# Layer 0's experts: slots of 256 rows at fixed places, then each expert's rest

## The chip, the cores and the metric

The kernel runs on one core of a Trainium2 chip. The metric is the device time of one execution in microseconds; 1060.14 us is the median of three runs before the change (1055.96 to 1061.04). TensorE is called PE, VectorE DVE, ScalarE ACT, GpSimd POOL and SyncE SP. Loads from device memory are issued mostly by SP, small stores by ACT, and transfers whose addresses come from a list of row numbers (indirect ones) by POOL.

## The reference

There are 3327 rows of 256 numbers, a symmetric 0/1 adjacency matrix, and two layers. Each layer is a graph step followed by a mixture of experts, and both are added to the rows. What is computed, cut to what matters here (`ln` is a layer normalisation):

```python
# layer 0
h = ln(x); a = (adj == 1)
x = x + (a @ h / a.sum(1)) @ W.T + b
h = ln(x)
probs = softmax(h @ gate_w + gate_b)                 # 16 experts
top_p, top_i = top_k(probs, 2); top_p /= top_p.sum(-1)
for each row and each of its two experts e:
    x += top_p * ((silu(h @ w1[e]) * (h @ w2[e])) @ w3[e])   # 256 -> 512 -> 256
# layer 1: a graph attention step, then 6 experts with a router of two layers, again 2 a row
```

Every row thus goes through two of the 16 experts: 6654 pairs of a row and an expert.

## The kernel before

The 3327 rows are 26 row tiles of 128 (the last one has 127). Seven chunks of four row tiles (the last has two) are the unit of all that follows the graph product.

**Graph step.** `graph` goes through blocks of chunks: 12, 8, 4 and 2 row tiles in each of the two layers (`GRAPH`). For each block it loads the adjacency matrix in groups (`load_adj`, L647 and L650: one row tile by the block's columns for wide blocks, three or six row tiles for narrow ones), makes a 0/1 mask of it on DVE (`mask_of`, L658), and multiplies (L772) into PSUM banks, two for each chunk. Three loads and three masks can be ahead (`AHEAD`). When a block is done its chunks are finished in steps (`finish`): multiplication with W (L715), layer normalisation, storing the rows (`store`) and the normalised rows, transposes (L732), the router (`choose`, L798) and `dispatch`. These steps are handed out over the groups of the next block, `steps` (7) for each chunk, two chunks at a time (`in_turn`). The last block's steps come after all matmuls.

**Lists.** `dispatch` picks two experts a row and writes the row's number and weight into that expert's list in device memory with indirect scatters (L361, two for each row tile). Its place is the number of earlier rows with that expert, kept in `seen`. Unused places of a list point to a spare row with weight zero. On one chunk of each layer a scatter waits until the one before the last has landed.

**Slots of layer 0.** A slot is 128 places of one expert's list. `slot_table` works out on DVE which expert and which place each slot has. Nine early slots need only the first block's rows; their table is made when the third block begins (`routed0`). The other 52 have a table made after the last chunk's `dispatch`. So 61 slots (`USUAL0`) are run in any case, and a branch (`asked`, `more`) leads to more of them when these don't suffice. For each slot SP reads a place from the table and loads 128 list entries (`places`, L543: `who`), POOL gathers the rows (`rows_in`, L551: `xg`), PE transposes them (`turned`, L568), then computes the hidden layer in 16 matmuls (`hidden0`, L938, two records each in the profile), ACT and DVE form silu times product (L942, L946), PE computes the output in four matmuls (`out0`, L954, eight records), DVE applies the row's weight (L957: `y`), and POOL adds the rows to the array in device memory (`rows_added`, L575: `xd`). Adds wait for each other. Weights are in two sets of buffers, one for even and one for odd slots; a slot loads its expert's weights (L536) only if its expert differs from that of the slot before last. `slots0` issues all this, gathers four slots ahead.

**The switch to layer 1.** Over the last eight slots `head1` reads back the first six row tiles and normalises them; `graph1_ahead` loads six groups of adjacency early. The remaining rows are read back (L1011) after the last add.

**Order.** The order of each engine's instructions is made by the framework from the program's order, the dependencies and its own estimate of durations. Explicit constraints are set by `issue_after` and by added dependencies; `in_order` keeps SP's loads for the slots in program order. In the profile the early slots run interleaved with the last block of layer 0's graph.

## Time and profile before

| | us |
|---|---|
| median of three runs | 1060.14 |
| the profiled execution | 1051.82 |
| its span, first to last instruction | 1049.9 |
| PE busy | 955.7 (91%) |
| PE's weight loads busy | 832.9 (79%) |
| DVE busy | 502.1 (48%) |
| POOL busy | 423.0 (40%) |
| ACT busy | 264.4 (25%) |
| hidden matmuls of layer 0's slots (L938), 1952 records | 351.5 busy, 283 ns each |
| output matmuls of layer 0's slots (L954), 488 records | 115.5 busy, 380 ns each |
| graph matmuls (L772), 1456 records | 351.5 busy, 395 ns each |
| mean granted clock of TensorE | 0.956 |

A line of the page's groups gives a source line, engine, operation and tile, the count, the busy time and the mean duration of one, and then how long the engine stood idle before such instructions and what ended the wait. Matmuls are pipelined: one starts while the one before still drains, so durations overlap, and the distance between starts tells what a matmul costs in a stream. In a timeline, neighbouring instructions of one kind are merged into a line: start, time from the first start to the last end, line, shape, count, and in brackets an idle time before it with the instruction or transfer that ended it.

### The profile page before, as it was taken

How to read it: one execution, taken by the hardware profiler on the slowest of the kernel's cores; microseconds unless marked ns; L12 is line 12 of the kernel's file. 1: busy time of each engine (PE TensorE's matmuls, PEld its weight loads, DVE VectorE, ACT ScalarE, POOL GpSimd, SP SyncE). 2: the span in 40 equal slices, each digit the busy share in tenths (PEclk: the TensorE clock that was granted, in tenths of full speed). 3: DMA queues.
4: the chain of work that ended last, by engine and by line, in shares of the span. 5: the costliest groups of instructions: out<-in, count | busy, mean ns of one | idle time of the engine just before them, and what ended most of it. 6: DMA issues, size and time to landing. Idle time of an engine off the chain costs nothing. (4 is left out here: it accounts for less than half of the span.)

```text
span 1049.9 us, 17490 instructions
## 1 busy us (share of the span) xinstructions
PE 955.7 (91%) x5404; PEld 832.9 (79%) x5404; DVE 502.1 (48%) x1839; ACT 264.4 (25%) x556; POOL 423.0 (40%) x400
## 2 busy tenths in 40 slices
PE   7899999799799999999999889999898688999980
PEld 5678877599699999999999878877677467888870
DVE  6667569166311222221212658676585641444653
ACT  3310211123111111111111524231222233444430
POOL 2040064055434445444443211002450476777742
PEclk9999899899989999999999989999999879999996
DMA  9987685969775766668767469857946666332365
GB/s 339 313 305 235 241 233 155 290 196 246 188 211 115 184 155 176 195 154 204 183 152 193 110 216 316 271 182 221 236 108 203 223 185 189 92 97 91 96 231 204
DMA packets 114716, 208.23 MB, mean 198 GB/s; under 512 B 32018, under 2 KB 68370, under 8 KB 114620
## 3 DMA queue, kind: packets, MB, share of 16 engines
q1 hardware_dynamic: 74590, 157.33, 47.2%
q0 software_dynamic: 21040, 31.61, 13.7%
q10 hardware_dynamic: 18990, 18.14, 5.6%
q8 instruction: 44, 0.72, 0.3%
q14 instruction: 52, 0.43, 0.1%
HBM read 232.46 MB, written 35.92 MB: 256 GB/s over the span
## 5 line engine op out<-in xcount | busy, mean ns | idle before, releaser
L772 PE MATMUL acc<-big,y 128*128 128x512 f32 (+2 forms) x1456 | 351.5, 395 | 28.4 <-DVE big L658 18.8
L772 PEld LDWEIGHTS acc<-big,y 128*128 128x128 f32 (+1 forms) x1456 | 267.9, 196 | 84.4 <-DVE big L658 7.8
L938 PE MATMUL acc<-xT,w 128*128 128x128 f32 x1952 | 245.0, 283 | 1.7 <-DMA w<-in_ffn_w 1.6
L938 PEld LDWEIGHTS acc<-xT,w 128*128 128x128 f32 x1952 | 238.7, 198 | 2.6 <-PE acc L938 1.3
L361 POOL DMA_INDIRECT list<-where,t_idx x104 | 110.1, 1059 | 187.0 <-DVE t_idx L357 74.8
L575 POOL DMA_INDIRECT xd<-y,who x61 | 95.9, 1572 | 178.8 <-DMA xd<-y,who 69.7
L658 DVE TENSOR_SCALAR big<-adj 128x1536 fp32r<-128x1536 int32 (+8 forms) x136 | 111.4, 824 | 97.4 <-DMA adj<-in_adj_t 67.9
L551 POOL DMA_INDIRECT xg<-hd,who x119 | 119.0, 1000 | 81.8 <-issue 30.8
L946 DVE TENSOR_TENSOR hid<-hid,acc 128x512 f32<-128x512 f32 x61 | 41.9, 688 | 204.8 <-PE acc L938 200.3
L954 PE MATMUL acc<-w,hid 128*128 128x256 f32 x488 | 115.5, 380 | 1.4 <-DVE hid L946 1.4
L954 PEld LDWEIGHTS acc<-w,hid 128*128 128x128 f32 x488 | 88.0, 190 | 11.3 <-DVE hid L946 1.8
L1119 ACT ACTIVATE h<-acc,v 128x256 f32<-128x256 f32 x116 | 54.9, 474 | 98.8 <-PE acc L1116 97.7
L583 POOL DMA_INDIRECT zd<-y,who x58 | 69.8, 1204 | 24.7 <-DVE y L1133 12.7
L570 ACT COPY xT<-mm 128x256 f32<-128x256 f32 (+1 forms) x74 | 32.2, 435 | 186.4 <-PE mm L568 155.8
L1116 PE MATMUL acc<-xT,v 128*128 128x256 f32 x232 | 62.8, 394 | 2.6 <-DMA v<-w1d 2.0
L1116 PE MATMUL acc<-h,v 128*128 128x256 f32 x232 | 60.5, 383 | 0.6 <-ACT h L1119 0.6
L1131 DVE TENSOR_TENSOR y<-acc,v 128x512 f32<-128x512 f32 x29 | 20.1, 691 | 83.1 <-PE acc L1128 83.1
L1128 PE MATMUL acc<-v,h 128*128 128x256 f32 x232 | 58.1, 394 | 0.1
L942 ACT ACTIVATE hid<-acc 128x512 f32<-128x512 f32 x61 | 36.4, 597 | 84.5 <-PE acc L938 83.0
L268 POOL TENSOR_TENSOR ln_var<-ln_var,half 128x2 f32<-128x2 f32 (+2 forms) x19 | 15.2, 803 | 102.7 <-DVE ln_var L266 91.8
L957 DVE TENSOR_SCALAR y<-acc,who 128x256 f32<-128x256 f32 x61 | 29.5, 484 | 52.1 <-PE acc L954 51.0
L1116 PEld LDWEIGHTS acc<-xT,v 128*128 128x128 f32 x232 | 43.8, 200 | 11.8 <-ACT h L1119 4.0
(264 smaller groups left out, 914.4 us busy)
## 6 DMA issues: line engine op xcount, KB each, us to landing
w<-in_ffn_w SPq DMA_DIRECT2D x183, 512.0 KB
adj<-in_adj_t SPq DMA_DIRECT2D x66, 768.0 KB
adj<-in_adj_t SPq DMA_DIRECT2D x50, 512.0 KB
v<-w1d SPq DMA_DIRECT2D x7, 898.0 KB
hd<-ln_h ACTq DMA_DIRECT2D x12, 512.0 KB
z<-zd SPq DMA_DIRECT2D x6, 1024.0 KB
adj<-in_adj_t SPq DMA_DIRECT2D x8, 765.0 KB
w_all<-w1d SPq DMA_DIRECT2D x6, 898.0 KB
```

The lines of the kernel that those rows point to most:

```text
L361: ins = nc.gpsimd.indirect_dma_start(out=rows_of[2 * (t0 + j) + i], out_offset=bass.IndirectOffsetOnAxis(ap=idx[:, i, j : j + 1], axis=0), ...
L551: last["pool"] = nc.gpsimd.indirect_dma_start(out=xg[:, h, :], out_offset=None, in_=of, in_offset=bass.IndirectOffsetOnAxis(ap=who[:, h, 1 ...
L575: nc.gpsimd.indirect_dma_start(out=to, out_offset=bass.IndirectOffsetOnAxis(ap=who[:, 0, 0:1], axis=0), in_=y, in_offset=None, compute_op= ...
L583: last["z"] = nc.gpsimd.indirect_dma_start(out=zviews[n * s + h], out_offset=bass.IndirectOffsetOnAxis(ap=who[:, h, 0:1], axis=0), in_=y[: ...
L658: last["mask"] = nc.vector.tensor_scalar(mask[:kr, :, :cols], a[:kr, :, :cols], value, None, op0=op)
L772: last["graph"] = nc.tensor.matmul(acc[c][k][:, :w], y[:kr, j, part, k * P : (k + 1) * P], mask[:kr, jj, i0 : i0 + w], start=(j == 0 and p ...
L938: nc.tensor.matmul(q[:, c, :], w[:, k, h0 : h0 + 2 * P - 1 : 2], xT[:, k, :], start=(k == 0), stop=(k == KD - 1))
L946: last["silu"], last["hid"] = silu, nc.vector.tensor_mul(hid, hid, ps[1])
L954: last["slot"] = nc.tensor.matmul(ps[:, :D], hid[:, c, :], w3[:, c // 2, c % 2, :], start=(c == 0), stop=(c == NC0 - 1))
L1116: ins = nc.tensor.matmul(ps[:, c, :], w[:, k, c : H1 : NC1], src[:, k, :], start=(k == 0), stop=(k == 1))
L1119: last["act"] = nc.scalar.activation(dst[:, c, :], ps[:, c, :], AF.Relu, bias=w1s[s % 3][:, BB + 2 * i + c : BB + 2 * i + c + 1])
L1128: nc.tensor.matmul(ps[:, h, :], h2[:, c, h * P : (h + 1) * P], w[:, c, :], start=(c == 0), stop=(c == NC1 - 1))
```

## The change

The graph blocks of layer 0 become 12, 4 and 10 row tiles (`GRAPH0`); layer 1 keeps its blocks. The first block's finishing steps may run on into the third block (`over`), and the third block's finishing steps are handed out beside the first slots (`beside`) instead of after the matmuls.

Slots of layer 0 get 256 places. After the 16 row tiles of the first two blocks, `filled` raises every expert's count to at least 256, so that its first 256 places are closed; places without a row keep pointing to spare rows. The first eight slots are the first 256 places of experts 0 to 7, at addresses known when the program is built; their lists are asked for at the 22nd group of the third block. After the last `dispatch`, `rank_table` ranks experts 8 to 15 by count, and then 0 to 7. Each of the former gets a slot for its first 256 places and one for its rest, each of the latter one for its rest. The rest's slot has a width by the rank: 256, 224, 224, 192, 192, 192, 160 or 160 rows (`WIDTHS`). That makes 32 slots. `spill_table` works out whether any rest is larger than its width; then the branch is taken, to two more slots and, inside it, to the others.

Weights are loaded once for a run of slots of one expert, 24 runs in all, unconditionally; hidden weights of the next run when a run starts, output weights when their own run starts. Hidden layers are computed in two halves of 256 hidden units, with the previous slot's output between them. Each slot's two adds go out without waiting for each other; both wait for both adds of the slot before. Buffers: three for `xg`, three half-size ones for `hid`, two for `y` (each now 256 rows), where there were five, two and four. The wait of a list scatter for the one before the last is now set on all chunks of the last block. `head1` and the ahead-of-time loads of layer 1 move with the slots' new numbers.

```diff
+    GRAPH0 = [CHUNKS[:3], CHUNKS[3:4], CHUNKS[4:]]
+    NE0 = sum(map(len, CHUNKS[:4]))
+    assert NE0 <= NF and len(GRAPH0[2]) <= 3
+    SA = 2 * P
+    HALF = E0 // 2
+    WIDTHS = [SA, SA - 32, SA - 32, SA - 64, SA - 64, SA - 64, SA - 96, SA - 96]
+    assert len(WIDTHS) == HALF and NP % SA == 0
+    USUAL0 = 4 * HALF
+    LATE0 = USUAL0 - 5
+    FEW0 = USUAL0 + 2
+    SLOTS0 = USUAL0 + (2 * N + E0 * (SA - 1 - WIDTHS[-1])) // SA
...
+        if not second_softmax and blk is GRAPH0[1][-1]:
+            filled(seen)
...
-                if blk is GRAPH[1][-1] and len(issued) > 1:
+                if len(issued) > 1 and (blk is GRAPH[1][-1] if second_softmax else blk in GRAPH0[2]):
...
+    def filled(seen):
+
+        ps = ps_mm.tile([P, 512], F32, name="mm")
+        nc.tensor.matmul(ps[:, :E0], ones_h, seen, start=True, stop=True)
+        short = work.tile([P, 2, E0], F32, name="f_short", bufs=1)
+        for h in range(SA // P):
+            nc.vector.tensor_scalar(short[:, h, :], ps[:, :E0], -1.0, float(SA - h * P), op0=OP.mult, op1=OP.add)
+        for h in range(SA // P):
+            nc.vector.scalar_tensor_tensor(seen, short[:, h, :], slot_p[:, 0:1], seen, op0=OP.is_gt, op1=OP.add)
...
+    def rank_table(seen):
+
+        ps = ps_mm.tile([P, 512], F32, name="mm")
+        nc.tensor.matmul(ps[:, :E0], ones_h, seen, start=True, stop=True)
...
+        return out, rank, rest
+
+    def spill_table(rank, rest, head):
...
     def in_turn(those):
 
-        now, those = those[:2], those[2:]
-        while now:
-            for i, one in enumerate(list(now)):
+        now = []
+        while those or now:
+            while those and len(now) < 2:
+                now.append(those.pop(0))
+            for one in list(now):
                 try:
                     next(one)
                     yield
                 except StopIteration:
                     now.remove(one)
-                    now += those[:1]
-                    those = those[1:]
 
...
+    def graph(name, blocks, prepare, value, op, wx, update, after, steps, routed, between=None, pools=None, ahead=(), ready=None, over={}, finish_with=None):
...
+            for b, block in enumerate(blocks):
...
+                    if (b, gi) in routed:
+                        routed[b, gi]()
...
-                    for _ in range(-(-left // (len(groups) - gi))):
+                    for _ in range(-(-left // max(1, over.get(b, len(groups)) - gi))):
...
-                post, left = in_turn([finish(*p) for p in parts]), steps * len(parts)
-            for _ in post:
-                pass
+                if not left:
+                    assert next(post, None) is None and not those
+                    post = in_turn(those)
+                those += [finish(*p) for p in parts]
+                left += steps * len(parts)
+            (finish_with or list)(post)
...
+    plan = [(e, None, 0, 0, SA) for e in range(HALF)]
+    for r in range(HALF):
+        plan += [(HALF + r, "rank", r, 1, SA), (HALF + r, "rank", r, 2, WIDTHS[r])]
+    plan += [(2 * HALF + r, "rank", HALF + r, 2, WIDTHS[r]) for r in range(HALF)]
+    assert len(plan) == USUAL0
+    plan += [(3 * HALF + i, "spill", i, 1, SA) for i in range(SLOTS0 - USUAL0)]
+
+    def places0(s):
+
+        run, table, row, col, _ = plan[s]
+        who = io.tile([P, 2, 3], I32, name="who", bufs=16)
+        if table is None:
+            src = lists[0][run * NP : run * NP + SA, :]
+        else:
+            with in_order():
+                at = nc.sync.value_load(early[table][row : row + 1, col : col + 1], min_val=0, max_val=E0 * NP)
+            src = lists[0][bass.ds(at, SA), :]
+        with in_order():
+            last["who"] = nc.sync.dma_start(who, src.rearrange("(h p) w -> p h w", p=P))
+        return who
...
-        early["table"], early["had"] = slot_table(E0, seen0, P, slot_p, first=EARLY0)
-        for s in range(EARLY0):
-            who[s] = places(early["table"], s, E0, lists[0], P)
+        for s in range(HALF):
+            who[s] = places0(s)
...
+    def load0_hidden(s):
+        run, table, row, _, _ = plan[s]
+        if table is None:
+            which[run] = slice(run, run + 1)
+        else:
+            with in_order():
+                which[run] = bass.ds(nc.sync.value_load(early[table][row : row + 1, 0:1], min_val=0, max_val=E0 - 1), 1)
+        with in_order():
+            for i, w in enumerate((ffn0_w1, ffn0_w2)):
+                load0(s, i, w[which[run]].rearrange("o (p k) h -> p (o k) h", k=KD))
+
+    def load0_out(s):
+        with in_order():
+            load0(s, 2, ffn0_w3[which.pop(plan[s][0])].rearrange("o (a p b) d -> p (o a) b d", p=P, b=2))
...
+    def hidden0(s, xT, half):
+        n, ps = plan[s][-1], []
+        for w in w0[plan[s][0] % 2][:2]:
+            q = bank(half, [P, 2, SA])
+            for c in range(2):
+                for k in range(KD):
+                    h0 = half * 2 * P + c
+                    last["slot"] = nc.tensor.matmul(q[:, c, :n], w[:, k, h0 : h0 + 2 * P - 1 : 2], xT[:, k, :n],
+                                                    start=(k == 0), stop=(k == KD - 1))
             ps.append(q)
-        hid = io.tile([P, NC0, P], F32, name="hid", bufs=2)
-        silu = nc.scalar.activation(hid, ps[0], AF.Silu)
-        if s >= EARLY0 + 4 and packs:
+        hid = io.tile([P, 2, SA], F32, name="hid", bufs=3)
...
+    def out0(s, hid):
+        w3 = w0[plan[s][0] % 2][2]
+        ps = bank(2, [P, 2, D])
+        for h, m in parts0(s):
+            for c in range(NC0):
+                nc.tensor.matmul(ps[:m, h, :], hid[c // 2][:, c % 2, h * P : h * P + m], w3[:, c // 2, c % 2, :],
+                                 start=(c == 0), stop=(c == NC0 - 1))
+        y = io.tile([P, 2, D], F32, name="y", bufs=2)
+        names = []
+        for h, m in parts0(s):
+            nc.vector.tensor_scalar(y[:m, h, :], ps[:m, h, :], weight(who[s], h)[:m, :], None, op0=OP.mult)
+            ins = nc.gpsimd.indirect_dma_start(
+                out=xd_of[2 + h] if s < USUAL0 else xd,
+                out_offset=bass.IndirectOffsetOnAxis(ap=who[s][:m, h, 0:1], axis=0),
+                in_=y[:m, h, :], in_offset=None, compute_op=OP.add,
+            )
+            if s < USUAL0:
+                waits(ins, [v for g, v in enumerate(x_added.get(s - 1, ())) if g != h])
+                if s == 0:
+                    waits(ins, x_stored[: len(GRAPH0[0]) + len(GRAPH0[1])])
+                if s == HALF:
+                    waits(ins, x_stored[len(GRAPH0[0]) + len(GRAPH0[1]) :])
+                names.append(ins.ins.name)
+        x_added[s] = names
...
-    graph("0", prepare0, 1.0, OP.is_equal, Later(0), update0, after0, 7, routed0, (operands_early, derived, derived_late))
-
-    table0 = slot_table(E0, seen0, P, slot_p, taken=early["had"], two=True, low=seen_head, late=LATE0 - EARLY0)
...
     def slots0(first, end):
+        usual = not first
+        for s in range(first - 3, end + 1):
+            if usual and s in AHEAD_AT:
+                graph1_ahead(AHEAD_AT.index(s))
+            if usual and s == HALF - 3:
+                early["rank"], *early["ranks"] = rank_table(seen0)
+            if usual and s == HALF + 4:
+                early["spill"] = spill_table(*early["ranks"], seen_head)
+            if usual and s == end - 2:
+                early["more"] = asked(early["spill"], 0)
+            if s == first - 1:
+                load0_hidden(first)
+            if first <= s < end and starts(s):
+                if next_run(s) < end:
+                    load0_hidden(next_run(s))
+                load0_out(s)
+            known = HALF if s < HALF - 3 else end
+            for i in range(max(who, default=-1) + 1, min(s + 4, known)):
+                who[i] = places0(i)
+            for i in range(max(xg, default=-1) + 1, min(s + 3, known)):
+                xg[i] = rows_in0(i)
             if first <= s + 1 < end:
+                xT[s + 1] = turned0(s + 1, xg[s + 1])
             if first <= s < end:
+                hid[s] = [hidden0(s, xT[s], 0)]
+                if usual:
+                    head1(2 * (s - LATE0))
+                yield
+            if first <= s - 1:
+                out0(s - 1, hid.pop(s - 1))
             if first <= s < end:
+                hid[s].append(hidden0(s, xT.pop(s), 1))
+                if usual and s == end - 1:
+                    spare = const.tile([P, 1], F32, name="spare")
+                    nc.scalar.activation(spare, half[:, 0:1], AF.Exp, bias=hid[s][1][:, 0, 0:1], scale=0.0)
+                if usual:
+                    head1(2 * (s - LATE0) + 1)
+                yield
+            elif s == first - 1:
+                yield
...
+    slots = slots0(0, USUAL0)
+
+    def beside(post):
+
+        for i, _ in enumerate(slots):
+            for _ in range(3 if i == 0 else 2):
+                if next(post, slots) is slots:
+                    return
+
+    graph("0", GRAPH0, prepare0, 1.0, OP.is_equal, Later(0), update0, after0, 7, {(2, 21): routed0, (2, 25): lambda: next(slots)},
+          (operands_early, derived, derived_late), over={1: 19, 2: 20}, finish_with=beside)
...
     with more(*early["more"]):
-        slots0(USUAL0, SLOTS0)
+        list(slots0(USUAL0, FEW0))
+        with more(*asked(early["spill"], 0, 5, "many")):
+            list(slots0(FEW0, SLOTS0))
```

## The prediction

> **What bounds the kernel now.** I read the page's busy shares first (PE 955.7 us, 91%; no other engine above 48%), then the busy time by stage, then PE's timeline where a stage shows idle time, then the queue that PE waited for there. By stage (the first column after the stretch is its length, then each engine's busy time with its instructions, the granted clock, the DMA share and GB/s):
>
> ```profile
> core 0: us, PE busy (x) PEld busy (x) DVE busy (x) ACT busy (x) POOL busy (x), PEclk, DMA share, GB/s
> 90.00:212.00 122.00, 111.32 (x526) 90.64 (x525) 73.45 (x340) 18.99 (x40) 32.59 (x30) 0.92 0.71 223
> 212.00:281.00 69.00, 68.46 (x513) 65.17 (x513) 42.13 (x227) 20.77 (x36) 38.41 (x36) 0.99 0.78 221
> 281.00:292.00 11.00, 2.42 (x12) 2.00 (x11) 0.66 (x2) 0.37 (x1) 6.11 (x5) 0.68 0.74 195
> 292.00:602.00 310.00, 306.86 (x2227) 294.62 (x2226) 75.71 (x169) 59.82 (x121) 133.36 (x103) 0.99 0.66 169
> ```
>
> Up to 90 us layer 0's first graph block runs, which the change leaves alone; 90 to 212 is its second and third, 212 to 281 the fourth with the nine early slots mixed in, 292 to 602 the late slots. PE is full in the slots and has two holes. PE's timeline at the first, at the second, and over one late slot:
>
> ```profile
> 183.60 4.60 PE L772 MATMUL acc<-big,y 128*128 128x512 f32 x19
> 195.58 6.50 PE L772 MATMUL acc<-big,y 128*128 128x512 f32 x19 [7.39 <-DVE big L658]
> ...
> 279.85 1.89 PE L954 MATMUL acc<-w,hid 128*128 128x256 f32 x8
> 290.32 0.70 PE L568 MATMUL mm<-ident,xg 128*128 128x128 f32 x2 [8.57 <-DMA xg<-hd,who]
> ...
> 298.26 0.39 PE L568 MATMUL mm<-ident,xg 128*128 128x128 f32 x2
> ...
> 585.45 1.89 PE L954 MATMUL acc<-w,hid 128*128 128x256 f32 x8
> 587.17 0.39 PE L568 MATMUL mm<-ident,xg 128*128 128x128 f32 x2
> 587.40 3.93 PE L938 MATMUL acc<-xT,w 128*128 128x128 f32 x32
> 591.17 1.89 PE L954 MATMUL acc<-w,hid 128*128 128x256 f32 x8
> ```
>
> Starts matter here, since a busy matmul overlaps the next: a late slot is 5.72 us (585.45 to 591.17), 3.77 for 32 hidden records, 1.73 for 8 output records, 0.23 for the transposes. So a pass costs 0.118 us at 128 columns and 0.216 at 256. The first hole waits for a mask, thus for an adjacency load on SP, the second for a gather. SP's queue at the first (start, time over all, issues):
>
> ```profile
> 150.88 15.34 SPq L647 DMA_DIRECT2D adj<-in_adj_t  x6
> 176.45 11.35 SPq L543 DMA_DIRECT2D who<-list  x9
> 187.90 1.80 SPq L647 DMA_DIRECT2D adj<-in_adj_t  x3
> ```
>
> Nine row-list loads stand between two adjacency loads: they wait for the list scatters to land, and then take some 1.2 us each, because each reads its address from a table. For 22 us no adjacency load goes out.
>
> **The change part by part.** All against the profiled execution, 1051.82 us (span 1049.9 and 1.9 around it); the median of the three timed runs, 1060.14, is 0.8% above it.
>
> *Slots of 256 rows.* Before, 61 x 128 = 7808 rows. After, 16 x 256 + 2 x 1600 (the widths' sum) = 7296 rows in 32 slots. The reference's router on its own inputs gives 324 to 511 rows an expert; with the first 256 places filled up, the rests are 132 to 255 and 140 to 200 in the two halves, and each fits its rank's width (the tightest: 255 in 256). So the usual 32 slots suffice. Hidden: 61 x 3.77 = 230.0 us becomes 7296/256 x 32 x 0.216 = 197.0. Output: every slot has two halves and a half moves 256 columns whatever its rows, so 61 x 1.73 = 105.5 becomes 64 x 1.73 = 110.7. Transposes: 61 x 0.23 = 14.0 becomes 14.7. Sum -27.1 us, on PE's path. That hidden passes run at 0.216 with 256 moving columns is seen in layer 1, which has this shape already:
>
> ```profile
> 930.46 1.89 PE L1128 MATMUL acc<-v,h 128*128 128x256 f32 x8
> 932.19 1.03 PE L1116 MATMUL acc<-h,v 128*128 128x256 f32 x4
> 933.05 1.03 PE L1116 MATMUL acc<-xT,v 128*128 128x256 f32 x4
> ```
>
> Four in 0.86 us. [...]
>
> *The second hole goes.* Late slots' tables need the last row tiles' routing, and early slots are too few to cover it. The chain ran from the last index (261.67, DVE) to the transpose at 290.32: 28.6 us. The hole cost 8.57 idle, and the first slot after it took 7.94 instead of 5.72 at a low clock: 10.8 us. After, eight early slots of 10.83 us (32 x 0.216 + 2 x 1.73 + 0.46) stand there, and the last block's finishing runs beside them: 87 us of cover instead of 51.
>
> *The first hole goes.* Row lists for the early slots are asked for at group 21 of the last block, behind most adjacency loads, and from fixed addresses: 8 x 0.35 us instead of 9 x 1.2 and a table. It cost 7.39 idle and 19 matmuls at 6.50 instead of 4.60: 9.3 us.
>
> The three together: -47.2 us. Against that:
>
> *The early slots' lists.* They now need chunks 2 and 3, whose steps end together at group 15: 16 scatters of 1.28 us on POOL (0.97 and 0.3 before each), 20.5, then 2.9 to the list load, 4.1 to the gather, 6.4 to the transpose (the distances at 276.96, 279.87, 283.95, 290.32): 33.9 us. Cover: ten groups of 2.16 us, and 6.2 us of finishing matmuls (32 L715 records at 1.55 for 8). Between 0 and 12 us; I take 4, somewhat under the difference of 6.1, since the first of the scatters can go while the step's other chunk still computes. Adjacency loads behind the list loads on SP: 0 to 7.4 (the old hole), I take 1, since nine table reads are gone.
>
> *The rank table's chain.* 28.6 us before, against two early slots (21.7) by the order of issue, three (32.5) if PE's order is drawn out: 0 to 9 us with the low clock; I take 2.
>
> *POOL.* The wait of each list scatter for the one before the last, on 8 scatters before, is now on 20, in the queue that also gathers and adds. Eight such scatters took 17.1 us (229.87 to 246.97) instead of 10.2. The queue stood for DMA there:
>
> ```profile
> 234.42 0.97 POOL L361 DMA_INDIRECT list<-where,t_idx  x1 [2.21 <-DMA list<-where,t_idx]
> ...
> 240.41 0.97 POOL L361 DMA_INDIRECT list<-where,t_idx  x1 [2.47 <-DMA list<-where,t_idx]
> ```
>
> For 20, 17 us more. Adds queued behind hold y, which has two buffers; then DVE's y and PE's banks wait. 0 to 17 us; I take 2, because two buffers are 21 us of slots. Adds themselves: one waits for both of the slot before, about 4.2 us after issue, in slots of 8 to 11 us: hidden.
>
> *Weights.* 24 runs of one or two slots, 1.5 MB each. A run's hidden weights have one slot (8.2 to 10.8 us) to land; before, a change of expert had 7.7 (two outputs, two transposes, a hidden), and PE waited 1.6 us for it in all. 0 to 8 us (1 us for each single-slot run at the end), I take 1. The packed copies on ACT's queue and the six ahead-of-time adjacency loads keep their number.
>
> *At no cost.* Tables: some 45 small DVE instructions of 0.15 to 0.3 us leave and as many come, beside PE (DVE is busy 76 of 310 us; uncovered about 9 us). Graph matmuls and masks are the same columns in other blocks. The question about more slots is asked two wide slots before the end (17 us) instead of four small (23), all five engines waiting for a table made at slot 12. *The end:* two adds instead of one behind the last slot, 1.9 us; loads of the remaining rows follow; 0 to 2, I take 1.
>
> Sum -47.2 + 11 = -36: 1016 beside the profiled execution, and **1024** beside the median, which is what I forecast.
>
> **The rivals.**
> 1. *New waits take the savings of the holes.* Everything above at its upper end but POOL's half: 12 + 7 + 9 + 9 + 4 + 2 = 43, of which about 30 can fall together, leaves -17: 1043. For it: POOL is in order and has more to wait for. Against: before, the mixed stage of 212 to 281 lost 0.5 us on PE with POOL at 38 of 69.
> 2. *Weight loads, not columns, set the pace of wide passes.* If hidden passes stood halfway, 0.167 us, that is another -45 us: 979. [...]
> 3. *Slower: the POOL chain decides.* Place: the 20 waiting scatters while slots run. If a pair waits long enough, adds come late, y stays full and PE stands still. The slack is 21 us, so 10 pairs have to cost 5.8 us more than a free pair (2.56) to eat 21 and the other 36; the longest wait seen is 4.09 (at 246.80). At 10 us a pair it is 1077.
> 4. *The slots don't suffice.* One row more than fits sends all engines through the extra slots: 2 x 10.8, a table and gather chain (10.5, from 279.87), and the first rows' normalisation again behind them (18.5, from 605.19 to 623.67): +51, thus 1075. The counts speak against it, by one row.
>
> [...]
>
> **How the numbers follow.** Forecast 0.62 (1010 to 1035), rival 1 0.19 (two thirds of it below 1045), rival 2 0.05, rival 3 0.05, rival 4 0.05, no change 0.04. The range reaches from no new waits (1060 - 47, and 7 for the spread of the runs) to the middle of rival 1: 1006 to 1045. Differences within 0.5%, about what a measurement of this kernel can tell from none, count as same: faster 0.85, same 0.05, slower 0.10.
>
> **What would show it.** Right: no idle above 5 us on PE between 90 us and the end of the slots; hidden passes at 0.216 us; slots ending near 565 us instead of 602; layer 1's graph and slots as long as now. Wrong: a gather or list that PE waits for at the start of slot 0 or 8; DVE's y waiting for an add; hidden passes held up by weights in the last eight slots; a taken branch to the extra slots.

## The result, and the profile after

The changed kernel takes 1028.97 us (median of four runs, 1025.44 to 1031.69). The kernel before took 1058.05 us in the same comparison. The ratio is 0.9725 with a 95% interval of 0.9675 to 0.9776: about 29 us or 2.75% faster. The forecast was 1024 us, with a range of 1006 to 1045. The profiled execution of the changed kernel took 1030.67 us (span 1028.9), against 1051.82 before. So the two profiles are 21 us apart, and not 29: the profiled execution of the kernel before was shorter than any of its four timed ones (1054.15 to 1061.04). What follows from the profiles explains 21 us.

The stages of the changed kernel, over the same stretches and with the same columns as before:

```profile
core 0: us, PE busy (x) PEld busy (x) DVE busy (x) ACT busy (x) POOL busy (x), PEclk, DMA share, GB/s
90.00:212.00 122.00, 111.02 (x596) 93.18 (x594) 69.92 (x315) 15.89 (x34) 40.58 (x38) 0.97 0.71 218
212.00:281.00 69.00, 64.03 (x322) 56.35 (x323) 37.27 (x162) 24.44 (x39) 24.95 (x24) 0.92 0.59 181
281.00:292.00 11.00, 10.93 (x61) 9.43 (x60) 6.79 (x34) 4.62 (x7) 7.47 (x7) 1.00 0.53 155
292.00:602.00 310.00, 298.35 (x1485) 260.23 (x1485) 88.37 (x251) 56.35 (x108) 146.31 (x115) 0.99 0.68 181
```

The stretch of 281 to 292, which was the second hole, is now full (10.93 busy of 11). But PE is not full in the others: 11 us are free in the first, 5 in the second at a clock of 0.92, and 12 in the fourth, which holds slot 8 and the end of the slots. PE's timeline shows where. It has the start of the slots, slot 8, and the last slots:

```profile
209.32 0.67 PE L1015 MATMUL mm<-ident,xg 128*128 128x128 f32 x2 [8.20 <-DMA xg<-hd,who]
212.05 0.70 PE L1015 MATMUL mm<-ident,xg 128*128 128x128 f32 x2 [2.06 <-DMA xg<-hd,who]
217.67 4.63 PE L797 MATMUL acc<-big,y 127*128 127x512 f32 x12 [4.91 <-DVE big L680]
...
319.16 0.70 PE L1015 MATMUL mm<-ident,xg 128*128 128x128 f32 x2 [5.79 <-DMA xg<-hd,who]
...
320.90 5.78 PE L1027 MATMUL acc<-xT,w 128*128 128x256 f32 x16
...
573.28 2.45 PE L1027 MATMUL acc<-xT,w 128*128 128x160 f32 x16
575.57 3.79 PE L1050 MATMUL acc<-w,hid 128*128 128x256 f32 x16
```

Both old holes are gone, and two new ones stand where their successors begin. At slot 0 PE waits 8.20 and 2.06 us for the gathered rows, and then 4.91 for a mask. At slot 8 it waits 5.79 for one half of the rows and 0.55 for the other, after 0.71 for a value of the second table, and the 16 passes after that take 5.78 us instead of 3.62, at a granted clock of 0.62 (318 to 327). The passes themselves cost what was expected: 16 hidden passes of 256 columns take 3.45 us between starts in the slot after that, 0.216 each, and 16 of 160 columns 2.29 us (573.28 to 575.57), one stall of 0.1 us among them. SP's queue at the first hole:

```profile
203.51 3.96 SPq L952 DMA_DIRECT2D who<-list  x8
...
208.56 0.88 SPq L672 DMA_DIRECT2D adj<-in_adj_t  x2
```

The adjacency loads before that end at 188.5. The eight list loads wait until 203.51 for the list scatters, and the last adjacency load stands behind them until 208.56. Its mask is what the third wait at slot 0 is for.

To see what these holes cost in all, PE's time from the last matmul of the first graph block to the first one of layer 1's graph is split in two. *Passes* is the sum over all matmuls of the median distance between starts for their shape. *Rest* is what is left: waits, low clock, small stalls.

| kernel | stretch, us | passes | rest |
|---|---|---|---|
| before | 515.6 | 475.6 | 40.0 |
| after | 490.8 | 450.7 | 40.1 |
| after, run again | 493.8 | 450.2 | 43.5 |

So the 24.8 us that this stretch became shorter are in the passes, and the holes were exchanged for holes of about the same size. (Which starts are counted into a median moves passes and rest by some 2 us against each other.) What is left of layer 1, from that first matmul to the end of the span, was 446.0 us (1049.9 - 603.9) and is 447.6 (1028.9 - 581.3). The first graph block ended at 88.3 us and ends at 90.5. Together that is -24.8 + 1.6 + 2.2, the 21 us between the profiles. Where the other 8 us between the medians lie, no trace shows.

### The profile page after: what moved, and what is told of

The parts are those of the page before. It is cut to its first block, busy times and chain, and to the rows that moved or that the text cites. A ratio compares the mean times of both kernels' runs of the same rounds, so it can differ in the third digit from the quotient of the medians.

```text
span 1028.9 us, 14333 instructions
## 1 busy us (share of the span) xinstructions
PE 929.3 (90%) x4505; PEld 782.0 (76%) x4505; DVE 497.6 (48%) x1824; ACT 260.8 (25%) x532; POOL 428.4 (42%) x408
## 5 line engine op out<-in xcount | busy, mean ns | idle before, releaser
L797 PE MATMUL acc<-big,y 128*128 128x512 f32 (+2 forms) x1456 | 341.2, 389 | 28.3 <-DVE big L680 19.8
L797 PEld LDWEIGHTS acc<-big,y 128*128 128x128 f32 (+1 forms) x1456 | 264.3, 193 | 85.7 <-ACT y L853 9.2
L1027 PE MATMUL acc<-xT,w 128*128 128x256 f32 (+3 forms) x1024 | 212.8, 361 | 0.0
L1027 PEld LDWEIGHTS acc<-xT,w 128*128 128x128 f32 x1024 | 186.4, 198 | 15.9 <-issue 3.1
L680 DVE TENSOR_SCALAR big<-adj 128x1536 fp32r<-128x1536 int32 (+6 forms) x130 | 111.5, 860 | 121.3 <-DMA adj<-in_adj_t 78.2
L1056 POOL DMA_INDIRECT xd<-y,who x64 | 99.0, 1547 | 65.2 <-DVE y L1055 19.2
L1050 PE MATMUL acc<-w,hid 128*128 128x256 f32 (+3 forms) x512 | 118.0, 381 | 0.7 <-DVE x_out L439 0.7
L1035 DVE TENSOR_TENSOR hid<-hid,acc 128x512 f32<-128x512 f32 (+3 forms) x64 | 40.1, 629 | 139.7 <-PE acc L1027 134.1
L1050 PEld LDWEIGHTS acc<-w,hid 128*128 128x128 f32 (+3 forms) x512 | 89.5, 178 | 20.7 <-issue 3.3
L1031 ACT ACTIVATE hid<-acc 128x512 f32<-128x512 f32 (+3 forms) x64 | 35.2, 550 | 202.6 <-PE acc L1027 195.9
L1262 DVE TENSOR_TENSOR y<-acc,v 128x512 f32<-128x512 f32 x29 | 20.1, 692 | 86.8 <-PE acc L1259 86.8
```

The costliest lines, as they stand in the source:

```text
L680: last["mask"] = nc.vector.tensor_scalar(mask[:kr, :, :cols], a[:kr, :, :cols], value, None, op0=op)
L797: last["graph"] = nc.tensor.matmul(acc[c][k][:, :w], y[:kr, j, part, k * P : (k + 1) * P], mask[:kr, jj, i0 : i0 + w], start=(j == 0 and p ...
L1027: last["slot"] = nc.tensor.matmul(q[:, c, :n], w[:, k, h0 : h0 + 2 * P - 1 : 2], xT[:, k, :n], start=(k == 0), stop=(k == KD - 1))
L1050: nc.tensor.matmul(ps[:m, h, :], hid[c // 2][:, c % 2, h * P : h * P + m], w3[:, c // 2, c % 2, :], start=(c == 0), stop=(c == NC0 - 1))
L1056: ins = nc.gpsimd.indirect_dma_start(out=xd_of[2 + h] if s < USUAL0 else xd, out_offset=bass.IndirectOffsetOnAxis(ap=who[s][:m, h, 0:1], a ...
```

## The experiments

The runs were made on several chips, on which the kernel before took 1056.7, 1096.9, 1084.2 and 1057.2 us. So ratios are compared across chips, and the stretch of the table above is given with each. On the second of these chips the kernel before spread from 1087 to 1112 us, so the ratios of the four kernels run there settle little by themselves. The passes of that stretch were the same on all chips for the same matmuls (449.9 to 451.0 us); what differed most was layer 1 behind it (477.3 us in one run on the second chip, against 447.6).

**The change once more.**

> The changed kernel once more, as the base that the edits below are held against on one chip. If the holes on PE belong to the kernel and not to one execution, the profile shows again about 15 us of idle time between 200 and 222 us and about 6 us at 313, and the time is 0.97 of before. If they were an accident of one execution, they differ by several us.

Measured: 1026.69 us, ratio 0.9731 (0.9692 to 0.9771). Waits at slot 0 of 8.18, 2.17 and 5.66 us; at slot 8 3.23 us (for a value of the second table, `x_out`) and 6.75. The two new holes are no accident of one execution, but their parts vary by 1 to 2.5 us.

**The list loads behind the last adjacency load.** Everything in `routed0` is called at the last group, after its mask instead of before its load, and the list loads are bound to the last adjacency load.

```diff
-                nc.sync.dma_start(a[lo:hi, 0, :cols], src[lo:hi, :])
+                last["adj"] = nc.sync.dma_start(a[lo:hi, 0, :cols], src[lo:hi, :])
...
-            who[s] = places0(s)
+            with tc.issue_after(last["adj"].ins):
+                who[s] = places0(s)
...
-    graph("0", ..., {(2, 21): routed0, (2, 25): lambda: next(slots)},
+    graph("0", ..., {(2, 25): lambda: (routed0(), next(slots))},
```

> Only SP's order is changed: the eight list loads of the early slots go out behind the last adjacency load of layer 0's graph, not ahead of it. Theory A (the hole at the start of the slots is two waits in a row: the row lists' chain of 10.3 us, from 200.8 to 212, and 4.9 us for the last adjacency load that stood behind the list loads on SP): the second wait goes, the first stays, 4 to 6 us faster than the changed kernel, hole about 10 us. Theory B (SP's order is the whole cause): the hole goes, 15 us faster. Theory C (weights of the first slot are late, and the waits only cover that): no change, PE waits for weights instead.

Measured: 1023.76 us, ratio 0.9676 (0.9622 to 0.973); stretch 485.4. PE's timeline at slot 0:

```profile
212.59 0.70 PE L1018 MATMUL mm<-ident,xg 128*128 128x128 f32 x2 [2.43 <-DMA xg<-hd,who]
212.94 4.55 PE L799 MATMUL acc<-big,y 127*128 127x512 f32 x12
```

The first wait, just before, is 8.26 us. The third is gone and the last graph group follows at once. So the wait for the mask came from the order on SP, and it cost 5 us of the stretch or more (490.8 and 493.8 with it).

**The first two blocks' steps handed out faster.** The first block's steps end in the second block, and the second block's by group 12 of the third.

```diff
-          (operands_early, derived, derived_late), over={1: 19, 2: 20}, finish_with=beside)
+          (operands_early, derived, derived_late), over={1: 10, 2: 12}, finish_with=beside)
```

> Only the handing out of the finishing steps is changed: all steps of the first block's chunks lie in the second block (spread over 10 groups, not 19), the second block's chunk is done by group 12 of the third block at the latest, not at group 15 together with the chunk before. Theory A: the sixteen list scatters on POOL, 22 us in one piece, are split and end some ten groups earlier, so the row lists are there in time; the hole of 15 us falls below 5, and the kernel is 8 to 15 us faster than the changed one, unless the second block now waits for DVE. Theory B (SP's order): the list loads still stand ahead of the last adjacency loads, but find their lists landed: the same gain. Theory C (first weights): no change.

Measured: 1028.89 us, ratio 0.9737 (0.9685 to 0.9788); stretch 491.3. The 8-us wait for slot 0's rows is gone (what is left there is 2.79, 1.96 and 0.49 for masks), and the time is the same. The finishing steps now lie close together in the third block, and there PE ran at half its clock for 10 us. One stretch and what PE did in it:

```profile
core 0: us, PE busy (x) PEld busy (x) DVE busy (x) ACT busy (x) POOL busy (x), PEclk, DMA share, GB/s
140.60:150.80 10.20, 10.20 (x33) 8.78 (x34) 3.87 (x15) 1.14 (x3) 7.05 (x7) 0.50 0.37 112
```

```profile
138.06 1.92 PE L757 MATMUL mm<-ident,ln_h 128*128 128x128 f32 x8 [1.65 <-ACT ln_h L275]
...
142.00 3.00 PE L825 MATMUL mm<-gw,aT 128*128 128x16 f32 x14
```

The lists can come in time; the price is paid earlier. That the router's matmuls of 16 columns bring the low clock on is suggested by their place, and not shown. The kernel before has the same twice: at 121.1 and 206.4 us, within two runs of 16 such matmuls, the clock falls to 0.50 for 6.8 us while PE is busy without a break. In the changed kernel, where 1.7 us of graph matmuls stand between the two runs (165.01 to 170.22), it stays at 1.00.

**No waits between the list scatters of the last three chunks.**

```diff
-                if len(issued) > 1 and (blk is GRAPH[1][-1] if second_softmax else blk in GRAPH0[2]):
+                if len(issued) > 1 and second_softmax and blk is GRAPH[1][-1]:
```

> Only the added waits between list scatters of layer 0's last three chunks are left out (the scatters write places of their own, and the first four chunks' scatters have no such wait). Theory A (at slot 8 PE waits for a chain that POOL holds up: it is busy without a break from 262 to 311 us, and 6.5 us of that are these waits): the hole of 5.8 us at 313 us and the low clock behind it, 8 us together, shrink by 6 to 8 us. Rival: the chain begins too late, with the last chunk's finishing steps, and POOL only follows: 0 to 2 us.

Measured: 1031.53 us, ratio 0.9806 (0.9736 to 0.9876), so not better; stretch 494.0. At slot 8 PE waits 2.92 and 5.73 us. The scatters went ahead without waits, and then the queue stood for something else. POOL's timeline:

```profile
296.09 1.54 POOL L1056 DMA_INDIRECT xd<-y,who  x1 [6.33 <-DVE k_rest L401]
...
299.79 1.02 POOL L363 DMA_INDIRECT list<-where,t_idx  x1 [0.30 <-DVE x_nt L422]
```

Two things show here. DVE was late (`k_rest` belongs to the rank table), and two adds stand ahead of the last four list scatters. Why DVE was late is in its own queue; in the changed kernel:

```profile
297.77 0.42 DVE L393 TENSOR_TENSOR y<-k_key 128x256 f32<-128x256 f32 x1 [5.25 <-DMA xd<-y,who]
298.11 0.16 DVE L359 CAST t_idx<-t_v 128x2 int32<-128x2 f32 x1
```

The rank table's comparison, for which all else was there at 292.02, is written into one of the two `y` buffers of the slots. It waits 5.25 us until an add has read that buffer, and the second index cast of the last chunk, without which the last scatters can't be issued, stands behind it.

**The comparison in the table's own PSUM bank.**

```diff
-        more_ = io.tile([P, 2, D], F32, name="y", bufs=2)[:, 0, : E0 * E0].rearrange("p (a b) -> p a b", b=E0)
+        more_ = ps[:, E0 : E0 + E0 * E0].rearrange("p (a b) -> p a b", b=E0)
```

> Only the place changes where the rank table's 16 x 16 comparison is written: the table's own PSUM bank instead of one of the two y buffers of the slots. In the two profiles of the changed kernel that comparison was issued 5 to 8 us late on VectorE, because the buffer was still being added to the rows, and the last chunk's second index cast stood behind it. Theory A (the shared buffer is the cause of the wait at slot 8): the cast comes 5 us or more earlier, TensorE's wait before slot 8's transposes falls from 5.8 and 6.8 us to under 2, the time to 1020 (1026.7 and 1029.0 for the changed kernel so far). Theory B (GpSimd's queue is the cause: 20 list scatters at 1.28 us and eight adds at 1.9 us between 275 and 312 us leave no room): the cast comes earlier, but the last four scatters start at the same time as now within 1.5 us, TensorE's wait stays above 4 us, the time within 1025 to 1030. Theory C (both in series, each covers the other): the wait falls by 2 to 3 us.

Measured: 1059.77 us where the kernel before took 1096.88, ratio 0.964 (0.9535 to 0.9746); stretch 496.3. The comparison no longer waits (`k_key` at 297.41, the comparison at 297.82, the cast at 298.16). But the last scatters are no earlier, and PE's wait before slot 8 is 7.31 us. POOL's timeline says why:

```profile
304.51 1.57 POOL L1056 DMA_INDIRECT xd<-y,who  x1 [2.54 <-DVE x_at L436]
306.38 1.57 POOL L1056 DMA_INDIRECT xd<-y,who  x1 [0.30 <-issue]
308.26 1.03 POOL L363 DMA_INDIRECT list<-where,t_idx  x1 [0.30 <-issue]
```

The index was ready at 298.16, the queue free at 301.97. POOL then stood 2.54 us for slot 3's output, issued its two adds, and came to the scatters at 308.26. So in this run it is neither the scratch buffer nor POOL's load, but the fixed order of POOL's queue. By the trace theory A fell; of theory B the effect held, and not the reason it gave. (The ratio's interval is too wide to tell the times of the two theories apart.)

**Both together, without the waits between scatters.** The two edits above in one kernel.

> The own place for the comparison and, together with it, no wait of one list scatter for the one before the last in the last three chunks. Without the waits alone the time had not fallen (1031.5). Theory C (two causes in series): only both together shorten GpSimd's stretch, the last four scatters start 4 us or more earlier than in the changed kernel (302.2 us there), TensorE's wait before slot 8 falls under 2 us, time 1017 to 1020. Theory A: no better than the own place alone. Theory B: four adds (7.6 us) still stand ahead of the last four scatters in GpSimd's order, so the wait stays above 4 us, time 1025 or more.

> The eight early list loads behind the last adjacency load on SyncE (1023.8 alone), the comparison's own place, and no waits between list scatters. If the three are independent: the list loads' 3 us and what the two others bring together, 1013 to 1017. If what the one saves at the start of the slots comes back as a wait at slot 8 (slots start earlier, the lists come no earlier): 1020 to 1024.

Measured: 1063.17 us, ratio 0.9677 (0.9598 to 0.9757), and with the list loads moved too 1054.46 us, ratio 0.9608 (0.9537 to 0.9679). In both, the wait before slot 8 is gone (no idle time over 0.45 us there). In both, another loss stands some 35 us earlier. A window of the second kernel:

```profile
core 0: us, PE busy (x) PEld busy (x) DVE busy (x) ACT busy (x) POOL busy (x), PEclk, DMA share, GB/s
275.00:288.00 13.00, 5.88 (x11) 3.13 (x12) 1.27 (x5) 0.60 (x1) 8.72 (x9) 0.64 0.02 1
```

Sixteen list scatters run here back to back, from 264.26 to 284.48. From 275 on the DMA engines moved 1 GB/s (132 in the 12 us before that), and PE's passes came one by one, with up to 1.64 us between them for which the profile names no cause. The granted clock was 0.64 in this window and 0.53 in the 12 us after it. What slot 8 no longer waits is lost here: the stretches are 499.4 and 493.1 us, no shorter than the plain change's. Theory C's wait fell, but not as it said. The last four scatters start 89.2 us (310.24 - 221.0) and 88.0 us (306.07 - 218.1) behind the end of the graph's matmuls, later than the changed kernel's 80.3 (302.21 - 221.9): the loss holds up PE's slots and the last index alike, and slot 8 comes too late to wait. The second kernel's ratio is the lowest of all, but its interval reaches to 0.9679, that of the list loads alone lies around 0.9676, and its stretch does not bear out a gain.

**The adds behind the scatters.** The comparison's own place, the waits between scatters as in the changed kernel, and another order on POOL: slot 3's adds are issued behind the last scatters and slot 4's behind the first gather.

```diff
+        if put_off:
+            with tc.issue_after(last["list" if s == HALF - 4 else "pool"].ins):
+                adds0(*put_off.pop())
+        if s in (HALF - 5, HALF - 4):
+            put_off.append((s, y))
+        else:
+            adds0(s, y)
```

> The comparison's own place, and GpSimd's order changed at slot 8: slot 3's two adds go behind the last four list scatters, slot 4's two behind the first gather. With the own place alone the last index cast came early (298.16) but the last scatters started at 308.26, because GpSimd stood 2.5 us for slot 3's y and then issued its two adds (3.8 us) ahead of them. Theory order (the fixed order of GpSimd's queue sets the wait at slot 8): the last scatters start within 3 us of the cast's end or right behind the scatters before them, 4 to 6 us earlier against the end of the graph's matmuls than in the run with the own place alone (82.8 us behind it there), TensorE's wait for slot 8's rows falls from 7.3 us to under 3, the ratio to the kernel before falls by 0.005 or more from the unchanged one's 0.973. Rival (GpSimd's work alone, 20 scatters and the gathers, fills the time): the wait stays above 5 us. Rival (late adds hold y): new idle time before output matmuls of slot 5 or 6.

Measured: 1044.47 us where the kernel before took 1084.16, ratio 0.9642 (0.9568 to 0.9717); stretch 489.0. POOL's queue, and PE's at slot 8:

```profile
300.08 0.97 POOL L363 DMA_INDIRECT list<-where,t_idx  x1 [1.35 <-DVE t_idx L359]
...
307.25 1.57 POOL L1070 DMA_INDIRECT xd<-y,who  x1 [0.30 <-issue]
```

```profile
316.07 3.62 PE L1029 MATMUL acc<-xT,w 128*128 128x256 f32 x16
319.52 0.63 PE L1017 MATMUL mm<-ident,xg 128*128 128x128 f32 x4
```

The scatters now wait for the cast itself. Against the end of the graph's matmuls they start 75.5 us behind it (300.08 - 224.6) instead of 82.8, slot 8's first gather 87.2 us instead of 92.1, and slot 8's transposes follow without a wait. That is theory order, and the stretch is 7.3 us shorter than with the comparison's own place alone (489.0 against 496.3; the changed kernel itself has 490.8 and 493.8). But the order brings the rows only about 5 us earlier, and the wait was 7.31: PE also comes to slot 8 3.0 us later here (94.9 us behind the end of the graph's matmuls, 91.9 before), after a wait of 2.95 us at 288.06 for which the profile names no cause. The new order without the own place was not tried.

**All of it, and the steps of the third block handed out faster.** The first kernel has the list loads' new order and the last edit's. The second adds this:

```diff
-            for _ in range(3 if i == 0 else 2):
+            for _ in range(4 if i == 0 else 3):
```

> The same, and the eight early list loads behind the last adjacency load on SyncE (0.968 alone, against 0.973). If both savings add up: TensorE idle between 90 us and layer 1 is what slot 0 waits for its rows (8.2 and 2.4) and little else, ratio 0.960 to 0.964. If the earlier start of the slots makes slot 8 wait again: 0.965 to 0.970.

> The list loads behind the adjacency loads, the comparison's own place, the adds behind the last scatters, and the finishing steps of the third block handed out three for each half slot instead of two (four for the first instead of three), so that the last dispatch comes earlier. In the run without the last of these TensorE still waited 4.0 us for slot 8's rows. If the last dispatch is what slot 8 waits for: the wait falls under 1 us and the ratio from 0.962 to about 0.958. If the scatters, now closer together, hold up the gathers of slots 5 and 6: a new wait of 2 us or more before their transposes, the ratio 0.96 to 0.97.

Measured: 1042.91 us where the kernel before took 1084.16, ratio 0.9619 (0.9526 to 0.9713), stretch 482.1; and 1017.11 us (1014.42 to 1020.5) where it took 1057.18, ratio 0.9639 (0.9597 to 0.9681), stretch 478.4. In the first the ratio is where the savings add up, but slot 8 waited 4.03 us again: without that loss of 2.95 us PE comes to it 90.6 us behind the end of the graph's matmuls, and the rows only at 94.6 (in the changed kernel 91.5 and 97.3). In the second:

```profile
208.15 0.67 PE L1020 MATMUL mm<-ident,xg 128*128 128x128 f32 x2 [8.32 <-DMA xg<-hd,who]
...
308.35 0.50 PE L1020 MATMUL mm<-ident,xg 128*128 128x128 f32 x2 [1.40 <-DMA xg<-hd,who]
```

Slot 8's wait is down to 1.40 and 1.08 us for the two halves of its rows (expected: under 1), and no new wait stands before slots 5 and 6. This is the fastest of the kernels by the stretch, 12 to 15 us under the change itself. Its time is about 0.9% under the change's by the ratios; the two intervals (0.9597 to 0.9681 and 0.9675 to 0.9776) still overlap by 0.0006. The wait for slot 0's rows remains.

**All slots 256 wide.**

```diff
-    WIDTHS = [SA, SA - 32, SA - 32, SA - 64, SA - 64, SA - 64, SA - 96, SA - 96]
+    WIDTHS = [SA] * HALF
```

> All 16 rests get 256 rows: 8192 rows instead of 7296, 896 more at 32/256 x 0.216 = 0.027 us each. Theory rows (a pass costs by its columns): +24.2 us, 1051, passes of the second and third part all at 0.216 us. Rival (weight loads set a floor for the narrower passes, which then cost no less): under +12 us. Rival (narrower slots lose time elsewhere, on gathers, adds and weights that have less to hide behind, and wide ones give that back): between +12 and +20 us.

Measured: 1075.81 us, ratio 0.9817 (0.9737 to 0.9897). On the same chip the kernel with the comparison's own place, which this one does not have, took 1059.77: 16.0 us less. Its stretch is 496.3 = 450.4 + 45.9, that of this kernel 512.5 = 473.3 + 39.2: +16.2, with +22.9 from the passes (expected 24.2 by the rows) and -6.7 from the rest. Against the changed kernel's own stretches it is +18.7 and +21.7. Most of what the rest gives back is in the late slots. From 330 us to their end the kernel with narrower slots has 49 small stalls of about 0.1 us each, 5.0 us together, between passes and at the seams of transposes, hidden and output matmuls; with all slots wide there are three, 0.3 us together. So the third theory held in size, and not in what it named: PE has no wait for gathers, adds or weights there. Narrow slots save, but give about a fifth of it (4.7 of 22.9) back in such stalls.

**Hidden passes of at most 128 columns.**

```diff
-                for k in range(KD):
-                    h0 = half * 2 * P + c
-                    last["slot"] = nc.tensor.matmul(q[:, c, :n], w[:, k, h0 : h0 + 2 * P - 1 : 2], xT[:, k, :n],
-                                                    start=(k == 0), stop=(k == KD - 1))
+                for h, m in parts0(s):
+                    for k in range(KD):
+                        h0 = half * 2 * P + c
+                        last["slot"] = nc.tensor.matmul(q[:, c, h * P : h * P + m], w[:, k, h0 : h0 + 2 * P - 1 : 2],
+                                                        xT[:, k, h * P : h * P + m], start=(k == 0), stop=(k == KD - 1))
```

> Hidden passes of at most 128 rows, everything else as in the changed kernel: 256 rows become 128 and 128, 160 become 128 and 32. Theory rows (a pass costs 0.118 us at 128 and by its columns below): 18 full slots at 32 x (2 x 0.118 - 0.216) = 0.64 us more, the 14 others about 0.3 us more each, together +16 us. Theory floor (a narrower pass than 128 costs no less than 0.118): the 14 others cost 1.5 us (224 rows), 2.3 (192) and 3.2 (160) more, together +44 us. Rival 2 of the prediction (wide passes are cheaper than their columns, towards 0.167 us): already against the changed kernel's rows, it would be +60 or more.

Measured: 1085.1 us, ratio 1.0031 (0.9969 to 1.0093): the whole gain is gone. The passes of the stretch are 494.8 us instead of 450.7: +44.1, which is what theory floor gives. So without wide passes nothing of the change's gain is left. A slot of 160 rows near the end, its passes of 128 and 32 columns in turn (the view merges both under the first shape):

```profile
607.26 7.72 PE L1028 MATMUL acc<-xT,w 128*128 128x128 f32 x64
614.82 3.82 PE L1051 MATMUL acc<-w,hid 128*128 128x256 f32 x16
```

64 passes in 7.56 us, 0.118 each, half of them with 32 columns.

## Why the prediction was right, and where it was not

The forecast of 1024 was 5 us under the time, and its sum of -36 against the measured -29 (1058.05 to 1028.97). Part of that nearness is luck: the sum was made on the profiled execution, where it gave 1016, and there the time came to 1030.67, 15 us more, with -21 instead of -36. What the traces bear out is the saving of the passes; the rest of the forecast, that two holes of 20 us go and 11 us of new waits come, failed in its second half. By its steps:

- *Slots of 256 rows*, -27.1: right. (The table ahead of the prediction has 351.5 us busy for the hidden matmuls before; the profile has 245.0, and 351.5 is the graph's. The prediction's 230.0 is made from starts and does not use it.) Passes cost 0.216 us at 256 columns, 0.189 at 224, 0.163 at 192 and 0.136 at 160, and all passes of the stretch together came down by 24.9. Not foreseen were the 5 us of small stalls between narrower passes, which count in the rest.
- *The first hole goes* and *the second hole goes*, -20.1: both went, as the windows show, but the rest of the stretch did not shrink at all (40.0 and 40.1). The terms against them were too small: 11 us taken, and some 26 measured in waits and low clock.
- *The early slots' lists*, 4 taken of 0 to 12: 10.3 us of waiting (8.20 and 2.06), and some 2 us of low clock behind it. The chain was sized right, even long: 29.5 us from the first scatter (179.81) to the transposes (209.32), against 33.9. The step that failed is the cover, the work that PE does while the chain runs. Of the 27.8 us counted, the 6.2 of finishing matmuls stand behind slot 0's transposes in PE's order (L740 from 226.42 on), and so does the last graph group. From 179.81 to the wait PE had 21.3 us of work, so 8.2 were left.
- *Adjacency loads behind the list loads*, 1 taken of 0 to 7.4: 4.91 and 5.66 us in two profiles, and gone when the order on SP was changed. The reason given, nine table reads fewer, was true (eight loads take 3.96 us now), and beside the point: the loads stand in SP's queue for the scatters, until 203.51.
- *The rank table's chain* and *POOL*, 2 each: 7.05 us of waiting at slot 8 and 2.2 of low clock after it; 10.2 of waiting in the second profile. The chain's length was right: 26.8 us from the first of the last chunk's index casts (292.35) to the transposes (319.16), against 28.6. Mis-sized was the cover again. PE had 21.0 us of work in that time, the two slots (21.7) that the prediction counted by the order of issue; it hoped for the third. For *POOL* the place was right and the mechanism was not. Priced were the waits of one scatter for another (eight of which took 18.2 us before, from 229.87 to the next start at 248.07, rather than 17.1); without them the time was no better. What counted was that slot 3's adds stand ahead of the last scatters in POOL's order, and that a scratch buffer of the slots delays the last cast. The two stood one behind the other: removing the buffer's wait alone moved nothing, and removing both brought the rows earlier by some 3 us against the changed kernel (94.6 instead of 97.3).
- *Weights*, *the end*: 1 each. No weight load is waited for in the last eight slots; layer 1's part grew by 1.6 us.

Of the signs named, those for a wrong forecast were partly there: a gather that PE waits for, at slot 0 and at slot 8, each over 5 us. The slots ended at 579 us instead of 565. The first rival (new waits take the savings of the holes) describes what happened: the new waits took all of the 20 us, where the rival had let them take about 30 (its sum has weights at 4, where the text's upper end is 8). At 1029 the time lies nearer the forecast; by the profiles, -21 lies nearer the rival's -17 than the forecast's -36. Rival 2, wide passes cheaper than their columns, is out: its 0.167 us, halfway between the 0.118 and the 0.216 of the rows before, is shown by no run, and the passes of 256 columns cost 0.216. No run shows weight loads setting the pace of wide passes. Rivals 3 and 4 left no trace: POOL's waits between scatters gained nothing when removed, and layer 1 follows the slots at once.

Idle gaps and the clock: windows put the granted clock at 0.50 from 205.8 to 222.9, around the waits at slot 0, and the 16 passes behind the 5.79-us wait at slot 8 cost 2.2 us more. Behind the 4.03-us wait of a later run they took 4.84 us instead of 3.62, at 0.51 from 312 to 315.5. In the kernel before, gaps of 7.39 and 8.57 us were followed by 1.9 and 2.2 us of loss. Shorter ones cost nothing in two places: in the last kernel, waits of 1.40 and 1.08 us (3.80 us from 308.2 at a clock of 1.00), and in the kernel before one of 1.92 us at 603.90 (8 us from 603 at 1.00). But two stretches of the run with the first two blocks' steps handed out faster lost time without a long gap ahead of them. Behind waits of 2.79 and 1.96 us, 48 graph matmuls took 10.93 us from start to start (204.58 to 215.51), some 1.5 us more than at the pace of 36 in 7.04 us in the changed kernel (170.22 to 177.26); and the 10 us at 0.50 had no idle gap over 1.65 us ahead of them. So one long idle gap is not the only way there, and these runs give no length from which a gap costs clock.

## What to carry to other kernels

When a chain is to be hidden behind other work, count as cover only what stands ahead of the waiting instruction in the order of its own engine, not all the work that exists at that time: here 21.3 us of the 27.8 counted, and 8.2 us of waiting. When a wait goes away and the time does not move, look in the in-order queue for what stands next to it: here a late cast and two adds stood one behind the other, and taking away the first alone gained nothing (PE waited 7.31 us, against 5.79 and 6.75). And a scratch tile borrowed from a ring of buffers borrows the ring's waits as well: 5.25 us here.

## What the runs showed of the hardware that was not expected

- The fp32 hidden passes of the slots cost no less below 128 columns. With 128, 96, 64 and 32 moving columns, in the run with split passes, the distance between starts was 0.118, 0.117, 0.117 and 0.118 us in the median; above, it goes by the columns (0.136 at 160, 0.216 at 256, 0.00084 us a column). At that price 0.118 us are some 140 columns, an estimate from these numbers: the 128-column passes of the kernel before pay for 140, and slots narrower than that would save nothing in these passes. It is no floor for all matmuls: most of the bf16 ones that count rows (L335, 6 to 48 columns) start 0.025 to 0.030 us apart in the same traces. In the kernel before, nearly all weight loads of the 128-column passes start 0.117 to 0.119 us apart too, one for each pass. Whether they set the pace is not shown: no run here varied the weights of a narrow pass.
- While sixteen list scatters ran without waits for each other, PE's passes came singly for 13 to 14 us, and the DMA engines moved 1 and 10 GB/s. It happened in the profiles of both kernels that had the comparison's own place and no waits, and not in the one that only had no waits (130 GB/s and PE busy all 12.00 us from 268 to 280). A similar stretch (30 GB/s over 9 us) is in the run with split passes, and a single wait of 2.95 us in the one with the adds behind the scatters; both have the waits. Idle DMA engines alone don't hold PE up: in the changed kernel they moved 7 GB/s from 271 to 277 us, and PE was busy all 6.00 us. What PE stood for is not in the profile, and the cause stays open.
- In the run with the first two blocks' steps handed out faster, PE ran at a granted clock of 0.50 for 10.2 us without an idle gap over 1.65 us before it, where matmuls of 16 columns lie close together, and twice for 6.8 us in the kernel before.
- Narrow slots had stalls of about 0.1 us at their seams (between passes, at transposes, between output matmuls): 49 from 330 us on, 5.0 us together, against three and 0.3 us with all slots wide. Why was not tried.
